# A four-layer graph network in one replayed schedule: one-hot rows partly by ScalarE, the first and last batch by halves, and a new order

## The chip, the cores and the metric

The kernel runs on one core of one Trainium2 chip. The core has five engines with queues of their own: TensorE (PE in the profile, its weight loads PEld), VectorE (DVE), ScalarE (ACT), GpSimd (POOL) and SyncE (SP). DMA transfers are issued from the queues of SP, ACT and POOL. The metric is device time in microseconds; before the change it is 2977.16 us, the median of three runs (2974.79 to 2977.79).

## The reference

There are 32 graphs (batches) of 512 nodes with 128 features, and a 0/1 adjacency of 512 x 512 per batch in which about one entry in 32 is set. Four layers follow each other, each as `x = x + layer(relu(layernorm(x)), adj)`:

```python
# layer 0: maximum over the neighbours
p = h @ (W1 - W2);  q = h @ W2
x = x + max_j( relu(p[i] + q[j] + b) * adj[i, j] )
# layer 1: four steps, each on all earlier features that it lists
src_agg = l2norm(adj, rows) @ (nodes @ ws + bs)
dst_agg = l2norm(adj, columns).T @ (nodes @ wd + bd)
nodes   = tanh(concat(src_agg, nodes @ wn + bn, dst_agg) @ wu + bu)
# layer 2
x = x + (adj / rowsum) @ (h @ weight) + bias
# layer 3: four steps of a gated unit
m = adj.T @ (h @ weight[l]);  r, z = sigmoid(...), sigmoid(...)
n = tanh(xn + r * hn);        h = (1 - z) * n + z * h
```

The output is the last x, 32 x 512 x 128 floats.

## The kernel before

**Staging.** `batch(b)` (L1222) records one batch: `load`, `prepare` (adjacency to bf16 `ab`, its transpose `at`, norms, tables), `gathers` (layer 0), `layer1` and `layer23`. Nothing is issued while it records; an object `Flow` (L279) notes each operation with its engine and what it reads and writes. Nearly every instruction of the profile is therefore issued from one line, L504, and is told apart by its tiles.

**Order.** `Flow.run` keeps up to AHEAD = 6 parts open (the three weight parts `first`, `rest`, `last`, and the batches) and issues operation by operation. Each operation has a due time: the place of its part times PACE, less the work that still depends on it, less a lead of its stage from the table LEADS (L40). Of the operations of an engine that could start first, the one with the earliest due time goes. The places of the weight parts are WEIGHTS, those of the batches their number, for the last five less LAST (L48, L1238). The result is one fixed order per engine, in which several batches lie interleaved; in the middle it repeats from batch to batch. Where the scheduler expects PE to have nothing for more than a microsecond it puts in filler matmuls (`spin`, L1232).

**Layer 0.** For each node the neighbours' rows of q are wanted. They are found in two ways: `pkey` and `top` (DVE max of eight) find up to seven of those that the second way leaves, whose rows POOL fetches from a table in HBM by indirect DMA (28 gathers a batch into `gm` and four buffers `G`), and DVE takes the maxima. The second way takes the first four neighbours in each half of a tile of 128 nodes: `ccd` holds running counts, DVE's `tensor_scalar` (L1070) makes from it a one-hot matrix `oh` of 128 x 1024 for each of four tiles (jt) and four slots (k), PE multiplies it with `qhl` into `pa` (L1073), and DVE keeps the running maximum `acc` (L1077): 16 one-hots and 32 products a batch. Then acc is transposed (`px`), joined with gm (L1080), and the layer's sum x1 is formed.

**Layer 1** (L1095): per step, `pf` transposes the features, `hi` (ACT) and `lo` (DVE) are their rounded part and the rest, `aggregate` (L910) multiplies both with at and an (the adjacency by rows), 16 matmuls of 512 columns, DVE scales the sums into `ag`, and `pu` collects the full-float products before a tanh on ACT. **Layer 2 and 3** (L1150): pg2, mT and po for layer 2; then per step of layer 3 two gates `pk` from h and from mT, the aggregate pg3 between them, phn and pxn, four operations on DVE and ACT (nn, tanh, product, sum to h), and the transposes `ph`. Every matmul, activation and vector operation here covers all 512 nodes.

**Buffers.** SBUF tiles are rings by tag: a new tile waits until the last use of the one before. PSUM's eight banks are shared by four users (`BANKS = (2, 1, 2, 1)`: layer 0's preparation, layer 1, layers 2 and 3, and the one-hot products), who keep these numbers and share the other two.

Of the kernel before, what the change touches and what calls it, by code (L numbers as in the profile page):

```python
# [32 lines left out]
CODES = ((0, 1), (P, 1), (2 * P, 2), (4 * P, 4))  # L33
NLEFT = 7
PACE = 45.28
SPACING = 1.8
AHEAD = 6
BANKS = (2, 1, 2, 1)

LEADS = {  # L40
    "prepare": -31.3, "counts": -26.1, "keys": -29.9, "rows": -0.7,
    "gather0": 21.0, "gather1": 4.8, "gather2": 6.6, "gather3": -2.7,
    "first": 14.9, "layer1": -15.8, "layer10": -31.7, "layer11": -34.7,
    "layer12": -17.6, "layer13": -49.5, "layer2": 17.3, "layer3": 7.8,
    "layer30": 58.6, "layer31": 78.0, "layer32": 36.2, "layer33": 30.6,
    "out": 18.1,
}
LAST = (0.0, 0.0, -0.31, -0.67, 0.62)  # L48
WEIGHTS = (-4.52, -3.22, -3.0)
# [548 lines left out]
class FastWeights:  # L598
# [5 lines left out]
    def __init__(self, nc, F, a, const, mid, ps):  # L604
        self.F, self.mid, self.ps = F, mid, ps
        self.NL3 = a["L3_gnn_weight"].shape[0]
        n = a["x"].shape[1]

        def fixed(shape, dtype, name):
            return const.tile(shape, dtype, name=name)  # L610

        ident = fixed([P, P], F32, "ident")
        make_identity(nc, ident)
        identb = fixed([P, P], BF16, "identb")
        nc.vector.tensor_copy(identb, ident)
        self.ident, self.identb = ident, identb
        self.mhalf = fixed([P, 8], F32, "mhalf")
        nc.gpsimd.memset(self.mhalf, -0.5)

        self.ones = fixed([P, P], F32, "ones")
        nc.gpsimd.memset(self.ones, 1.0)
        ltf = fixed([P, P], F32, "ltf")
        nc.gpsimd.affine_select(
            ltf, self.ones, pattern=[[1, P]], compare_op=ALU.is_ge, fill=0.0, base=0,
            channel_multiplier=-1,
        )
        nc.gpsimd.memset(ltf[0:HP, HP:P], 0.0)  # L630
        self.lt = fixed([P, P], F32R, "lt")
        nc.vector.scalar_tensor_tensor(self.lt, ident, NBASE, ltf, ALU.mult, ALU.add)
        self.ltk = fixed([P, P], BF16, "ltk")
        nc.vector.tensor_scalar(self.ltk, self.lt.bitcast(F32), KEY, None, ALU.mult)
        self.code = fixed([P, n // P, P], BF16, "code")
        icode, code = fixed([P, n // P], I32, "icode"), fixed([P, n // P], F32, "fcode")
        for t, (first, step) in enumerate(CODES):
            nc.gpsimd.iota(
                icode[:, t : t + 1], pattern=[[1, 1]], base=first, channel_multiplier=step
            )  # L640
        nc.vector.tensor_copy(code, icode)
        for t in range(n // P):
            nc.vector.tensor_scalar(
                self.code[:, t, :], ident, code[:, t : t + 1], None, ALU.mult
            )


        self.sign = fixed([P, 2], F32, "sign")
        nc.gpsimd.memset(self.sign[:, 0:1], -1.0)
        nc.gpsimd.memset(self.sign[:, 1:2], 1.0)  # L650
        nc.gpsimd.memset(self.sign[0:4, 0:1], 1.0)
        nc.gpsimd.memset(self.sign[0:4, 1:2], 0.0)
        self.nc, self.a, self.const, self.n = nc, a, const, n
# [32 lines left out]
    def rest(self):  # L686
# [38 lines left out]
        for i in range(NL1):  # L725
# [4 lines left out]
            for k, nm in enumerate(("ws", "wn", "wd")):  # L730
# [8 lines left out]
                F.vec.tensor_copy(wt, pt[:, 0:ch, :])  # L739
# [25 lines left out]
    def last(self):  # L765
# [14 lines left out]
        F.vec.tensor_copy(w3t, pt[:, 0:NL3, :])  # L780
        self.gh, self.gm = [], []
        for l in range(NL3):
            for nm, dst in (("hh", self.gh), ("ih", self.gm)):
# [9 lines left out]
                if nm == "hh":  # L793
                    F.vec.tensor_copy(t, pg[:, 0:3, :])
                else:
                    gt = self.temp("xn2", f"gt_{l}")[:, 0:3, :]
                    F.vec.tensor_copy(gt, pg[:, 0:3, :])
# [19 lines left out]
def fast(ctx: ExitStack, tc: tile.TileContext, a: dict, out: bass.AP, bad):  # L817
# [47 lines left out]
    def norm(s, xt, tag):  # L865
# [13 lines left out]
        xn = F.tile(mid, [P, NT, P], F32, tag=f"xn{s}", name=f"xn_{tag}")  # L879
# [14 lines left out]
    def sbuf_parts(s, src, tag):  # L894

        hi = F.tile(mid, [P, NT, P], F32R, tag=f"hi{s}", name=f"hi_{tag}")
        F.act.copy(hi, src)
        lo = F.tile(mid, [P, NT, P], F32R, tag=f"lo{s}", name=f"lo_{tag}")
# [3 lines left out]
    def parts(s, src, tag):  # L902

        hi = F.tile(mid, [P, NT, P], F32R, tag=f"hi{s}", name=f"hi_{tag}")
        F.act.copy(hi, src)
        lo = F.tile(mid, [P, NT, P], F32R, tag=f"lo{s}", name=f"lo_{tag}")
        F.vec.tensor_sub(lo, src, hi.bitcast(F32))
        return hi, lo

    def aggregate(s, two, m, name):  # L910

        pg = pst(s, name)
        hi, lo = two
        for jt in range(NT):
            F.mm(flat(pg), hi[:, jt, :], m[:, jt, :], start=(jt == 0), stop=False)
            F.mm(flat(pg), lo[:, jt, :], m[:, jt, :], start=False, stop=(jt == NT - 1))
# [3 lines left out]
    def prepare(b, xt, af):  # L920
# [16 lines left out]
        at = F.tile(big, [P, NT, N], F32R, tag="at", name=f"at_{b}", bufs=3)  # L937
# [112 lines left out]
    def gathers(b, at, ccd, qhl, pn, tab, idx, has, dinv):  # L1050
# [15 lines left out]
        for jt in range(NT):  # L1066
            F.lead = LEADS[f"gather{jt}"]
            for k in range(1, KSLOT + 1):
                oh = F.tile(big, [P, 2, N], F32R, tag="oh", name=f"oh_{b}_{jt}_{k}", bufs=3)
                F.vec.tensor_scalar(oh, ccd[jt], NBASE + k, None, ALU.is_equal)  # L1070
# [24 lines left out]
    def layer1(b, x1, an, at, dinv):  # L1095
# [14 lines left out]
        feat = {"h": hT}  # L1110
        agg = {}
        new = "h"
        for i in range(NL1):
# [3 lines left out]
            if i:  # L1117

                pt = transposed(1, feat[new], f"pf_{b}_{i}")
                two = parts(1, pt, f"{b}_1_{i}")  # L1120
            ag = F.tile(mid, [P, 2, N], F32, tag="ag" + {"f2": "f1"}.get(new, new), name=f"ag_{b}_{i}")
            for k, m in ((0, at), (1, an)):
                pg = aggregate(1, two, m, f"pg_{b}_{i}_{k}")
                F.vec.tensor_mul(ag[:, k, :], flat(pg), rbc[:, k, :])
            agg[new] = ag
            pu = pst(1, f"pu_{b}_{i}")
            F.mm(flat(pu), W.b8[:, i, :], rows, start=True, stop=False)
            late = []
            for c, nm in enumerate(names):
                F.mm(flat(pu), w[:, 1, c, :], flat(feat[nm]), start=False, stop=False)  # L1130
                for k in range(2):
                    if nm == new:
                        late.append((c, k))
                        continue
                    F.mm(flat(pu), w[:, 2 * k, c, :], agg[nm][:, k, :], start=False, stop=False)
            for c, k in late:
                F.mm(flat(pu), w[:, 2 * k, c, :], ag[:, k, :], start=False, stop=(k == 1))
# [3 lines left out]
            F.act.activation(fi, pu, AF.Tanh, bias=W.bu[:, i : i + 1])  # L1141
# [8 lines left out]
    def layer23(b, x2, an, at, dinv):  # L1150
        xn = norm(2, x2, f"{b}_2")
        two = sbuf_parts(2, xn, f"{b}_2")
        F.pool.tensor_add(x2, x2, W.b2.unsqueeze(1).to_broadcast([P, NT, P]))
        pg = aggregate(2, two, at, f"pg2_{b}")
        mT = F.tile(mid, [P, NT, P], F32, tag="mT", name=f"mT2_{b}")
        F.act.copy(mT, pg)
        po = pst(2, f"po_{b}")
# [8 lines left out]
        xn = norm(2, x3, f"{b}_3")  # L1166
        two = sbuf_parts(2, xn, f"{b}_3")
        pt = transposed(2, xn, f"pt_{b}_3")
        h = F.tile(mid, [P, NT, P], F32, tag="hg", name=f"h_{b}_3")
        F.act.copy(h, pt)  # L1170
        for l in range(W.NL3):
            F.lead = LEADS[f"layer3{l}"]
            gates = []
            for k in range(2):
                pk = pst(2, f"pk_{b}_{l}_{k}")
                F.mm(flat(pk), W.gh[l][:, k, :], flat(h), start=True, stop=False)
                gates.append(pk)
            pg = aggregate(2, two, an, f"pg3_{b}_{l}")
            mT = F.tile(mid, [P, N], F32, tag="mT", name=f"mT_{b}_{l}")
            F.act.copy(mT, flat(pg))  # L1180
            for k in range(2):
                F.mm(flat(gates[k]), W.gm[l][:, k, :], mT, start=False, stop=True)
                g = F.tile(mid, [P, N], F32, tag=f"gate{k}", name=f"gate{k}_{b}_{l}")
                c = 3 * l + k
                F.act.activation(g, flat(gates[k]), AF.Sigmoid, bias=W.bsum[:, c : c + 1])
                if k == 1:

                    zc = F.tile(mid, [P, N], F32, tag="zc", name=f"zc_{b}_{l}")
                    F.pool.tensor_scalar(zc, g, -1.0, 1.0, ALU.mult, ALU.add)
                gates[k] = g  # L1190
            r, z = gates
            c = 3 * l + 2
            phn = pst(2, f"phn_{b}_{l}")
            F.mm(flat(phn), W.gh[l][:, 2, :], flat(h), start=True, stop=True)
            nn = F.tile(mid, [P, N], F32, tag="nn", name=f"nn_{b}_{l}")
            F.vec.scalar_tensor_tensor(
                nn, flat(phn), W.bhh[:, c : c + 1], r, ALU.add, ALU.mult
            )
            pxn = pst(2, f"pxn_{b}_{l}")
            F.mm(flat(pxn), W.gm[l][:, 2, :], mT, start=True, stop=True)  # L1200
            F.vec.tensor_add(nn, flat(pxn), nn)
            F.act.activation(nn, nn, AF.Tanh, bias=W.bih[:, c : c + 1])

            F.pool.tensor_mul(z, flat(h), z)
            hn = F.tile(mid, [P, NT, P], F32, tag="hg", name=f"h_{b}_{l}")
            F.vec.tensor_mul(nn, nn, zc)
            F.vec.tensor_add(flat(hn), z, nn)
            h = hn
            pt = transposed(2, h, f"ph_{b}_{l}")
            if l + 1 < W.NL3:  # L1210
                two = parts(2, pt, f"{b}_3_{l}")
        F.lead = LEADS["out"]
        xo = F.tile(mid, [P, NT, D], F32, tag="mT", name=f"xo_{b}")
# [24 lines left out]
    places = [b - LAST[max(0, b - B + len(LAST) - 1)] for b in range(B)]  # L1238
# [474 lines left out]
```

## Time and profile before

| what | value |
|---|---|
| median of three runs | 2977.16 us |
| the profiled execution | 2976.68 us, its span 2975.0 us |
| PE busy | 2861.7 us, 96% of the span |
| DVE busy | 2393.3 us, 80% |
| ACT busy | 1216.1 us, 41% |
| POOL busy | 1819.8 us, 61% |
| filler matmuls among PE's | 257, 69.7 us |
| HBM read and written | 164.32 and 17.96 MB |

How to read it: the groups of instructions give operation, output and inputs by the names in the program, with the shapes; the timelines give start, duration, engine, operation and, in brackets, how long the engine sat idle before and what ended it. Durations of PE's matmuls overlap, so the distance of two starts says what one costs. The windows give the busy time of each engine in a stretch, in the order PE, PEld, DVE, ACT, POOL, then the granted clock of PE as a share, the DMA engines' share and GB/s.

### The profile page before, as it was taken

The numbers are of one execution on the slowest core, as the hardware profiler recorded it, in microseconds if no ns is written. First come the engines' busy times: TensorE is split into PE (matmuls) and PEld (weight loads), VectorE is DVE, ScalarE is ACT, GpSimd is POOL, SyncE is SP. The second block draws the span as 40 slices with busy tenths as digits, with TensorE's granted clock in tenths as the row PEclk, the third lists the DMA queues.
The fourth block names the chain that finished last, engine by engine and source line by source line (L and its number), as shares of the span: only waits on it lengthen the run. The fifth ranks groups of instructions, "written<-read, shape, count | busy, mean of one in ns | idle before, by whom it ended". The sixth has DMA issues, their size and how long they took to land.

```text
span 2975.0 us, 37664 instructions
## 1 busy us (share of the span) xinstructions
PE 2861.7 (96%) x11490; PEld 1752.8 (59%) x11490; DVE 2393.3 (80%) x5363; ACT 1216.1 (41%) x2528; POOL 1819.8 (61%) x2005
## 2 busy tenths in 40 slices
PE   7789999999999999999999999999999999999997
PEld 4455556666666666666666666666666666655553
DVE  6978878988888898888889888888988888887532
ACT  3333434434444443444444344444434444433322
POOL 3666766666666666666666666666666666654411
PEclk9989999999999999999999999999999999999999
DMA  7553334334334333333443333344333334321200
GB/s 171 109 94 71 63 76 86 82 74 83 62 65 85 86 78 77 75 65 69 86 86 78 78 74 65 70 85 86 77 79 74 64 72 85 67 54 43 33 4 5
DMA packets 191266, 218.43 MB, mean 73 GB/s; under 512 B 30376, under 2 KB 139600, under 8 KB 191056
## 3 DMA queue, kind: packets, MB, share of 16 engines
q0 software_dynamic: 47104, 92.34, 22.5%
q1 hardware_dynamic: 73768, 63.63, 7.3%
q10 hardware_dynamic: 70184, 59.98, 6.5%
q8 instruction: 93, 1.52, 0.2%
q14 instruction: 117, 0.96, 0.1%
HBM read 164.32 MB, written 17.96 MB: 61 GB/s over the span
## 4 chain that ended last, share of the span: by engine, by line
PE 78%; DVE 12%; issue 4%; DMA 2%; ACT 2%; POOL 2%; DVEq 0%; SPq 0%; ACTq 0%; POOLq 0%
PE pg L504 23%; PE pu L504 18%; PE pk L504 15%; PE pa L504 6%; PE pxn L504 4%; PE phn L504 4%; DVE acc L504 3%; PE pkey L504 2%; PE ph L504 2%; PE pf L504 1%; DVE nn L504 1%; DVE qhl L504 1%; PE pt L504 1%; DVE oh L504 1%; DVE x L504 1%
## 5 line engine op out<-in xcount | busy, mean ns | idle before, releaser
L504 POOL DMA_INDIRECT G<-qtab,idx x768 | 840.8, 1095 | 574.5 <-DVE gm L504 461.5
L504 DVE TENSOR_TENSOR acc<-acc,pa 128x512 f32<-128x512 f32 x992 | 673.6, 679 | 146.3 <-PE pa L504 134.2
L504 PE MATMUL pa<-oh,qhl 128*128 128x512 f32 x1024 | 472.1, 512 | 10.8 <-DVE acc L504 6.6
L504 PE MATMUL pg<-an,hi 128*128 128x512 f32 x1024 | 458.8, 448 | 2.0 <-DVE lo L504 1.6
L504 PE MATMUL pu<-ag,w 128*128 128x512 f32 x896 | 449.3, 595 | 1.5 <-DVE ag L504 1.3
L504 PE MATMUL pg<-an,lo 128*128 128x512 f32 x1024 | 432.8, 424 | 0.0
L504 DVE TENSOR_SCALAR oh<-ccd 128x1024 fp32r<-128x1024 bf16 x512 | 392.2, 783 | 13.6 <-PE pa L504 12.6
L504 PE MATMUL pg<-at,lo 128*128 128x512 f32 x640 | 296.7, 464 | 0.6 <-POOL lo L504 0.5
L504 PE MATMUL pg<-at,hi 128*128 128x512 f32 x640 | 287.7, 449 | 6.9 <-ACT hi L504 3.2
L504 PEld LDWEIGHTS pa<-oh,qhl 128*128 128x128 f32 x1024 | 194.2, 191 | 143.9 <-issue 43.6
L504 DVE TENSOR_TENSOR gm<-gm,G 128x128 f32<-128x128 f32 x768 | 258.6, 338 | 5.5 <-DMA G<-qtab,idx 4.6
L504 PE MATMUL pk<-h,g_hh 128*128 128x512 f32 x512 | 258.4, 608 | 1.8 <-ACT h L504 1.1
L504 ACT ACTIVATE xn<-x,shift,rstd 128x128 f32<-128x128 f32 x512 | 211.6, 484 | 107.5 <-POOL shift L504 107.5
L504 PEld LDWEIGHTS pg<-an,hi 128*128 128x128 f32 x1024 | 192.7, 188 | 97.0 <-issue 49.0
L504 PEld LDWEIGHTS pg<-an,lo 128*128 128x128 f32 x1024 | 193.0, 188 | 85.9 <-issue 42.0
L504 PE MATMUL pk<-mT,g_ih 128*128 128x512 f32 x512 | 241.7, 594 | 1.1 <-ACT mT L504 1.1
L504 PEld LDWEIGHTS pu<-ag,w 128*128 128x128 f32 x896 | 169.5, 190 | 118.1 <-issue 82.8
L504 ACT ACTIVATE gate<-pk,bsum 128x512 f32<-128x512 f32 x256 | 175.7, 686 | 147.8 <-PE pk L504 144.5
L504 POOL TENSOR_TENSOR rstd<-rstd,mhalf 128x4 f32<-128x4 f32 x128 | 144.1, 1126 | 138.0 <-DVE shift L504 135.9
L504 ACT COPY mT<-pg 128x512 f32<-128x512 f32 x160 | 93.7, 586 | 328.3 <-PE pg L504 324.0
L504 DVE TENSOR_TENSOR ag<-pg,rbc 128x512 f32<-128x512 f32 x256 | 174.5, 683 | 42.8 <-PE pg L504 39.7
L504 ACT CAST hi<-ph 128x512 fp32r<-128x512 f32 x96 | 56.3, 586 | 365.2 <-PE ph L504 362.2
(169 smaller groups left out, 5135.2 us busy)
## 6 DMA issues: line engine op xcount, KB each, us to landing
af<-in_adj_dram ACTq DMA_DIRECT2D x32, 1024.0 KB
ccd<-cc SPq DMA_DIRECT2D x512, 64.0 KB
an<-in_adj_dram POOLq DMA_DIRECT2D x128, 256.0 KB, 3.7
x<-in_x_dram ACTq DMA_DIRECT2D x64, 256.0 KB
rbc<-scal SPq DMA_DIRECT2D x32, 512.0 KB
G<-qtab,idx POOLq DMA_INDIRECT x768, 3.8
qtab<-qn SPq DMA_DIRECT2D x128, 64.0 KB
out_dram<-xo ACTq DMA_DIRECT2D x32, 256.0 KB
```

Source lines behind the costliest of these rows:

```text
L504: op.fn(*(real(v) for v in op.args), **{k: real(v) for k, v in op.kw.items()})
```

## The change

- **One-hots.** In batches 0, 1 and 2, the last two, two and one of the four slots of each tile are made on ACT by two activations (`far = |ccd - (64 + k)|`, then `relu(1 - far)`) instead of one DVE operation.
- **Weights.** Four kinds of copies out of PSUM in the weights' preparation go from DVE to ACT.
- **Halves.** Layer 1 of the first and the last batch, and layer 3 of the last, work in two halves of 256 nodes: the aggregates, the products, the activations and the vector operations are cut in two; the aggregate still sums over all nodes.
- **Buffers.** The last batch's tiles of layers 2 and 3 lie in tags of layer 0 (table LATE), its `at` in the tag of `af`, and its PSUM tiles count as those of user 0. BANKS becomes (1, 1, 2, 1).
- **Order.** PACE, all LEADS, LAST and WEIGHTS are new, and the first three batches are shifted by FIRST.

```diff
+ONACT = (2, 2, 1, 0)
-PACE = 45.28
+PACE = 45.33
-BANKS = (2, 1, 2, 1)
+BANKS = (1, 1, 2, 1)
 LEADS = {
-    "prepare": -31.3, "counts": -26.1, "keys": -29.9, "rows": -0.7,
-    "gather0": 21.0, "gather1": 4.8, "gather2": 6.6, "gather3": -2.7,
-    "first": 14.9, "layer1": -15.8, "layer10": -31.7, "layer11": -34.7,
-    "layer12": -17.6, "layer13": -49.5, "layer2": 17.3, "layer3": 7.8,
-    "layer30": 58.6, "layer31": 78.0, "layer32": 36.2, "layer33": 30.6,
-    "out": 18.1,
+    "prepare": -25.4, "counts": -39.2, "keys": -29.6, "rows": -14.9,
+    "gather0": 7.4, "gather1": -2.0, "gather2": -7.1, "gather3": -19.7,
+    "first": 4.7, "layer1": -35.8, "layer10": -41.4, "layer11": -66.8,
+    "layer12": -31.3, "layer13": -62.8, "layer2": 19.7, "layer3": 106.4,
+    "layer30": -29.1, "layer31": 140.3, "layer32": 106.2, "layer33": 6.1,
+    "out": -31.3,
 }
-LAST = (0.0, 0.0, -0.31, -0.67, 0.62)
-WEIGHTS = (-4.52, -3.22, -3.0)
+FIRST = (0.49, 0.03, 0.25, 0.0)
+LAST = (0.0, -0.55, 0.49, -2.35, -2.71)
+WEIGHTS = (-2.59, -2.36, -5.92)
+
+LATE = {
+    "xn2": ("xn0", 1), "hi2": ("qn", 1), "lo2": ("gm", 1), "mT": ("acc", 1), "hg": ("hT0", 1),
+    "gate0": ("pn", 2), "gate1": ("ccd", 6), "zc": ("ccd", 6), "nn": ("ccd", 6),
+}
...
-                F.vec.tensor_copy(wt, pt[:, 0:ch, :])
+                F.act.copy(wt, pt[:, 0:ch, :])
...
-        F.vec.tensor_copy(w3t, pt[:, 0:NL3, :])
+        F.act.copy(w3t, pt[:, 0:NL3, :])
...
-                    F.vec.tensor_copy(t, pg[:, 0:3, :])
+                    F.act.copy(t, pg[:, 0:3, :])
...
-                    F.vec.tensor_copy(gt, pg[:, 0:3, :])
+                    F.act.copy(gt, pg[:, 0:3, :])
...
-    def aggregate(s, two, m, name):
+    def aggregate(s, two, m, name, c=slice(0, NT)):
 
         pg = pst(s, name)
+        out = flat(pg if c.stop - c.start == NT else pg[:, 0 : c.stop - c.start, :])
         hi, lo = two
         for jt in range(NT):
-            F.mm(flat(pg), hi[:, jt, :], m[:, jt, :], start=(jt == 0), stop=False)
-            F.mm(flat(pg), lo[:, jt, :], m[:, jt, :], start=False, stop=(jt == NT - 1))
+            v = m[:, jt, c.start * P : c.stop * P]
+            F.mm(out, hi[:, jt, :], v, start=(jt == 0), stop=False)
+            F.mm(out, lo[:, jt, :], v, start=False, stop=(jt == NT - 1))
         return pg
...
-        at = F.tile(big, [P, NT, N], F32R, tag="at", name=f"at_{b}", bufs=3)
+        home = ("af", 1) if b == B - 1 else ("at", 3)
+        at = F.tile(big, [P, NT, N], F32R, tag=home[0], name=f"at_{b}", bufs=home[1])
...
-                F.vec.tensor_scalar(oh, ccd[jt], NBASE + k, None, ALU.is_equal)
+                if k > KSLOT - ONACT[min(b, len(ONACT) - 1)]:
+
+                    far = F.tile(big, [P, 2, N], BF16, tag="far", name=f"far_{b}_{jt}_{k}")
+                    F.act.activation(far, ccd[jt], AF.Abs, bias=W.slot[:, k : k + 1])
+                    F.act.activation(oh, far, AF.Relu, bias=W.ones[:, 0:1], scale=-1.0)
+                else:
+                    F.vec.tensor_scalar(oh, ccd[jt], NBASE + k, None, ALU.is_equal)
...
+        step = NT // 2 if b in (0, B - 1) else NT
+        cuts = [slice(t, t + step) for t in range(0, NT, step)]
...
+            for j, c in enumerate(cuts):
+                for k, m in ((0, at), (1, an)):
+                    pg = aggregate(1, two, m, f"pg_{b}_{i}_{k}_{j}", c)
+                    F.vec.tensor_mul(
+                        ag[:, k, cols[j]], flat(cut(pg, slice(0, step))), rbc[:, k, cols[j]]
+                    )
...
     def layer23(b, x2, an, at, dinv):
+        own = dict(LATE) if b == B - 1 else {}
+        s = 0 if own else 2
...
+        step = NT // 2 if own else NT
+        cuts = [slice(t, t + step) for t in range(0, NT, step)]
...
+                F.vec.tensor_add(cut(nn, c), vx, cut(nn, c))
+                F.act.activation(
+                    cut(nn, c), cut(nn, c), AF.Tanh, bias=W.bih[:, n : n + 1]
+                )
+
+                F.pool.tensor_mul(cut(z, c), cut(h, c), cut(z, c))
+                F.vec.tensor_mul(cut(nn, c), cut(nn, c), cut(zc, c))
+                F.vec.tensor_add(cut(hn, c), cut(z, c), cut(nn, c))
+                for t in range(c.start, c.stop):
+                    F.tr(pt[:, t, :], hn[:, t, :], W.ident)
...
-    places = [b - LAST[max(0, b - B + len(LAST) - 1)] for b in range(B)]
+    places = [
+        b - FIRST[min(b, len(FIRST) - 1)] - LAST[max(0, b - B + len(LAST) - 1)] for b in range(B)
+    ]
```

## The prediction, made blind

> **What bounds the kernel now.** I read the page's busy line first, then stretches of the span, then the timelines of the two ends.
>
> ```profile
> PE 2861.7 (96%) x11490; PEld 1752.8 (59%) x11490; DVE 2393.3 (80%) x5363; ACT 1216.1 (41%) x2528; POOL 1819.8 (61%) x2005
> L528 PE MATMUL spin<-code,identb 128*128 128x512 bf16 x257 | 69.7, 408 | 8.2 <-DVE code L643 5.4 <-DVE acc L504 2.7
> ```
>
> PE is busy 96%, but 257 of its matmuls are fillers (spin) that compute nothing. Stretches, columns: window, width, PE, PEld, DVE, ACT, POOL busy, granted clock, DMA share, GB/s:
>
> ```profile
> 0.00:45.00 45.00, 32.41 (x172) 18.24 (x173) 19.39 (x58) 17.32 (x54) 6.25 (x31) 0.92 0.59 171
> 45.00:110.00 65.00, 50.74 (x268) 30.26 (x267) 60.68 (x142) 19.83 (x51) 46.35 (x52) 0.92 0.79 148
> 110.00:175.00 65.00, 55.07 (x223) 30.89 (x222) 58.95 (x138) 19.93 (x46) 43.29 (x49) 0.92 0.50 101
> 1500.00:1600.00 100.00, 98.67 (x388) 60.51 (x386) 87.11 (x186) 43.24 (x91) 65.49 (x73) 1.00 0.41 85
> 2793.00:2894.00 101.00, 98.28 (x332) 54.83 (x332) 38.62 (x85) 33.42 (x59) 22.78 (x25) 1.00 0.04 10
> 2894.00:2966.00 72.00, 59.82 (x217) 29.12 (x215) 21.21 (x55) 18.09 (x31) 13.78 (x15) 0.98 0.02 6
> ```
>
> Three regimes. In the middle PE sets the pace: the output of one batch follows the last by 86.95 us (821.85 to 908.80 in the DVE timeline). From 45 to 175 us DVE is the full engine (93 and 91%), ACT stands at 30%. At the end only one dependent chain is left. Full-rate steps of matmuls (start to start in the timeline) are 0.23 us for 512 columns in rounded float, 0.86 for 512 in full float (two records); with them the program holds about 2,672 us of real PE work, so some 300 of the 2,975 are lost: about 128 before 400 us, 4 to 5 in each 100 us of the middle, 50 in the last 185.
>
> The start in the timelines of ACT and DVE (start, duration):
>
> ```profile
> 9.10 0.40 ACTq L504 DMA_DIRECT2D af<-in_adj_dram  x1
> 16.18 0.29 DVE L504 TENSOR_TENSOR shift<-b0r,low 128x128 f32<-128x128 f32 x1 [10.79 <-ACT low L504]
> 21.55 0.29 DVE L504 COPY wt<-pwt 128x128 f32<-128x128 f32 x1 [2.10 <-PE pwt L504]
> 21.75 2.28 DVE L504 SCALAR_TENSOR_TENSOR junk<-af 128x2048 bf16<-128x2048 f32 x1
> 44.57 0.17 DVE L504 TENSOR_SCALAR idx<-row 128x28 int32<-128x28 int32 x1
> 109.45 0.68 DVE L504 TENSOR_TENSOR gm<-gm,px 128x512 f32<-128x512 f32 x1
> 174.85 0.68 DVE L504 TENSOR_TENSOR gm<-gm,px 128x512 f32<-128x512 f32 x1
> ```
>
> The adjacency of batch 0 is asked for at 9.10, its first use on DVE stands behind weight copies; batch 0's neighbour maximum ends at 109.45, batch 1's at 174.85. The end, PE's timeline:
>
> ```profile
> 2893.19 0.66 PE L504 MATMUL px<-ident,f 128*128 128x128 f32 x4 [0.35 <-ACT f L504]
> 2894.12 4.48 PE L528 MATMUL spin<-code,identb 128*128 128x512 bf16 x20
> 2914.88 1.98 PE L504 MATMUL pk<-h,g_hh 128*128 128x512 f32 x4 [0.38 <-ACT h L504]
> 2956.42 1.98 PE L504 MATMUL pk<-mT,g_ih 128*128 128x512 f32 x4 [0.28 <-ACT mT L504]
> 2959.10 2.75 PE L528 MATMUL spin<-code,identb 128*128 128x512 bf16 x12
> 2962.68 0.63 PE L504 MATMUL ph<-ident,h 128*128 128x128 f32 x4 [0.83 <-DVE h L504]
> ```
>
> Layer 2 of batch 31 takes 21 us (2893.9 to 2914.9) with almost nothing beside it, then four steps of layer 3 take 12.0 us each.
>
> **Part 1, the start: 20 us off (8 to 30).**
> Off DVE go the copies of weights (12 wt, 1 w3t, 4 gt, 4 g_hh: 0.2 to 0.6 us a step, 8.1 us in all) and 20 one-hots (8, 8, 4 in batches 0, 1, 2; consecutive starts in this stage are 0.60 apart: 12 us). Adding up the DVE instructions in the built order with their steps from the timeline, what stands ahead of batch 0's last neighbour maximum falls from 76.7 to 53.4 us (31 instead of 40 running maxima, 8 instead of 24 one-hots); ahead of batch 1's from 134.3 to 108.0, batch 2's 183.2 to 162.1, batch 3's 240.0 to 215.4, batch 4's 299.3 to 280.6. About 20 us less DVE work stays off.
> The path: af is now the first transfer on ACT's queue, ahead of ten weight transfers; on SP four weight transfers of 64 to 192 KB move ahead of w12, which `low` needs. ACT's first operation was held to 14.58 by its own queue and I leave it there; low and shift then stay near 16, and junk follows shift at once: 16.5 instead of 21.75, 5 us. The indices came at 44.57 behind junk of batch 1 (2.28), three one-hots (1.9) and two copies (0.8), which now stand later: 34.5, 10 us earlier in all. From there to the maximum took 64.9 us around 58.7 of DVE steps; now 42.8 stand there, and the 28 gathers become the limit. They took 55 us between issues; with four buffers and 5.2 us to landing (the DMA view of 40 to 110 us) a round of four needs about 7 us: 8 issues at 1.35 and 20 at 1.7, and one landing, 50 us. So the maximum comes at 85 instead of 109, and batch 1's, some 60 us of gathers later, near 148 instead of 175.
> ACT gains 40 operations on 128x1024: no row has that shape. Below, the gate on 512 elements (0.69); above, two of them (1.37); near twice, less one overhead, 1.05: 42 us over 200, with 8 of copies on the 30% it has. The 20 pairs fit beside DVE's running maxima, which they feed; priced at 1.37 they still do. If ACT answers late, PE's pa waits and the maxima behind it.
> How much of the 24 us reaches the end: PE is not full until batch 2 is under way, so its stages move up with the maxima; but waits on PE itself and the half clock (clock 0.92 above) also lie there. I take 20; the ends are 5 to 8 (the gathers hold) and 30.
>
> **Part 2, the end: 19 us off (8 to 26).**
> In the built order the transposes that open layer 2 of batch 31 (px) now stand before the last two steps of layer 3 of batch 30, which have buffers of their own beside it. PE work behind that point: 49.2 us, it was 33.8. The 15.3 us of batch 30 now lie inside the 21 us of batch 31's layer 2, which stretches a little as PE alternates: 2 us lost, 13 won.
> Halves in layer 3: a step is 7.4 us of PE and 4.6 of waiting. The 0.72 between aggregate and pk goes (the other half's aggregate, 1.0 us, covers it); the four operations between pxn and ph (0.70, 0.73, 0.90, 0.70 and their gaps, 3.3 in the chain) run on 256 columns; the qn row, 0.42 for 256 against 0.68, makes that 1.9. That would be 2.1 a step, but the order shows 7, 13, 7, 11 fillers between pxn and ph where 11, 12, 12, 12 stood: two steps hardly improve. I take 2 us twice and 0.7 twice, 5.4.
> Check by fillers: behind batch 31's neighbour maximum 111 stood, now 49; 12 fillers went with a hole of 3.4 us, so 62 fewer are 17 us. At the low end the halves give nothing and the overlap 8.
> Cost of halves on PE: full-float ones halve exactly (pq, 256 columns, 216 ns a record against 429). Rounded ones: nearest is the 128x128 transpose, each with its own weights, 0.109 a step; I price a half at 0.123, 0.016 us more per whole: 160 of them 2.6 us, b8 and the rest to 5.9, two thirds of it in holes. I charge 2. Upper end 0.23 per half, no gain at all from halving: 37 us more PE work, of which some 15 would show.
> TensorE: Matmul & The Clock Gate, Part 3 (The mechanism), says that weight loads run beside matmuls only in other row groups. By it each half would add a load of 107 ns (same page, LDWEIGHTS), an estimate of 34 us for 320 halves, and the time would come near 2955. The trace disagrees: loads of 188 ns sit inside steps of 0.23, and transposes with new weights each follow at 0.109.
>
> **Part 3, the middle: 5 us off (25 off to 20 on).**
> The leads and PACE reorder every batch; the work is the same (DVE 66.5 us of steps per batch in both). PE has 2.5 to 4 us of holes per batch. Work between producer and consumer in the built orders, per batch: pf after pu in step 0, 0.7 to 1.3 us; pk after pt, 0.7 to 1.1 (it stalled 0.2); ph after pxn in the last step, 5.6 to 7.2 (a stall of 0.75 stood before ph); against that px after pu 1.7 to 1.3, ph after pxn in the others 0.2 to 0.4 shorter. Nothing falls below its chain (f 0.68 and a semaphore). I take 0.2 us a batch over 25; the ends are 1 us a batch gained and 0.8 lost.
>
> **Sum.** 2976.7 (the profiled execution: span 2975.0 and 1.7 around it; 0.5 under the median of the runs shown) - 20 - 19 - 5 + 2 = 2934.7. I say 2936.
>
> **Rivals.**
> A, *the gathers or the transfers hold the start.* For it: DMA stands at 0.79 from 45 to 110, and POOL waits for landings. Against: most of its waits for a gather are for DVE's gm. Start 6 instead of 20: 2949.
> B, *the middle's new order loses.* The one case that ends slower: a stall between pxn and ph (DVE and ACT answer later behind other operations) in each batch. It decides from (20 + 19 - 2) / 25 = 1.5 us a batch; at 2.5 the sum is 2976.7 - 37 + 62.5 = 3002. Against: no filler stands in the middle of the new order, as in the old, and the distances are like.
> C, *the chain of the last batch stays as long* because both halves go through DVE one by one and batch 30's work delays it. Tail 8: 2946.
> D, *everything holds and the middle gains 1 us a batch*: 2915.
>
> **How the numbers follow.** Forecast 0.50, A 0.15, B 0.11, C 0.12, D 0.09, no change by losses that cancel 0.03. The range 2910 to 2968 leaves out most of B and a little of the rest. Under 0.2% (6 us) the runs, 3 us apart, cannot tell from no change; by it faster 0.86, same 0.03, slower 0.11.
>
> **What would show it.** Right: junk of batch 0 before 18 us, its neighbour maximum near 85, batch 1's near 150, DVE under 85% in 45 to 175, about 192 fillers; px of batch 31 with xo of batch 30 20 us later; layer 3 steps of 10 to 11.3. Wrong: an unchanged 109 (gathers), batches more than 88 us apart in the middle (order), or steps of 12 at the end (halves).

## The result and the profile after

The changed kernel is slower: 3000.04 us, median of four runs (2997.48 to 3001.75), against 2977.15 (2974.79 to 2977.79) for the kernel before beside it; the ratio is 1.0078 (1.0060 to 1.0095). The forecast was 2936; a middle that loses, the outcome of its rival B, is what came. The profiled execution took 2999.38 us, its span 2997.7: 22.7 more than the span before.

Where the time lies is read from the outputs. `xo` on DVE is the last work of a batch. Its first instruction for batches 3 and 24, from DVE's timeline of the changed kernel (start, duration):

```profile
555.02 0.35 DVE L511 SCALAR_TENSOR_TENSOR xo<-ph,mcol,x 128x128 f32<-128x128 f32 x1
2424.46 0.35 DVE L511 SCALAR_TENSOR_TENSOR xo<-ph,mcol,x 128x128 f32<-128x128 f32 x1
```

The same two of the kernel before:

```profile
561.13 0.60 DVE L504 SCALAR_TENSOR_TENSOR xo<-ph,mcol,x 128x128 f32<-128x128 f32 x2
2386.02 0.60 DVE L504 SCALAR_TENSOR_TENSOR xo<-ph,mcol,x 128x128 f32<-128x128 f32 x2
```

Over the 21 batches between, that is 89.02 us a batch instead of 86.90: 2.12 us lost in each. Cut at the outputs of batches 2 and 24:

| part | before | after | difference | forecast |
|---|---|---|---|---|
| start to xo of batch 2 | 472.3 | 466.8 | -5.5 | -20 |
| from there to xo of batch 24 | 1913.7 | 1957.7 | +44.0 | -5 |
| from there to the end of the span | 589.0 | 573.2 | -15.8 | -19, and +2 for halves on PE |

The end did what was said, the start a quarter of it, and the middle has the wrong sign. The start's 5.5 is uncertain by some 3 us: in two other traces with the same starts (`tail` and `notail` below) the first row is 474.9 for the old one and 465.7 for the new. The page and the windows of the changed kernel, with the columns of the prediction's windows:

```profile
PE 2864.6 (96%) x11706; PEld 1783.8 (60%) x11725; DVE 2388.7 (80%) x5363; ACT 1272.8 (42%) x2622; POOL 1850.4 (62%) x2018
```

```profile
45.00:110.00 65.00, 49.92 (x267) 30.72 (x271) 47.05 (x116) 45.13 (x94) 42.25 (x53) 0.95 0.86 162
110.00:175.00 65.00, 54.86 (x300) 40.05 (x303) 55.22 (x134) 41.20 (x74) 43.58 (x47) 0.97 0.49 101
1500.00:1600.00 100.00, 97.25 (x383) 59.45 (x382) 85.63 (x185) 40.76 (x83) 62.78 (x69) 1.00 0.35 70
```

The page's busy shares barely move: 96% for PE in both. The loss is seen in the third window: 97.25 instead of 98.67 us of PE and 383 instead of 388 matmuls in 100 us. Which waits these are, from the waits of PE between 600 and 2340 us (engine, tile, whom it waited for: us in total, times, longest). The changed kernel:

```profile
PE pq L511 <- DVE acc L511: 11.4, 19, 0.6
PE po L511 <- DVE x L511: 10.1, 19, 0.9
PE px L511 <- DVE acc L511: 6.7, 20, 2.0
PE pk L511 <- ACT mT L511: 5.2, 20, 0.3
PE ph L511 <- DVE h L511: 4.6, 19, 0.3
PE pu L511 <- DVE acc L511: 1.8, 3, 0.6
```

The kernel before, the whole list:

```profile
PE ph L504 <- DVE h L504: 10.9, 18, 0.6
PE po L504 <- DVE x L504: 10.3, 20, 0.5
```

Before, 21.2 us in 20 batches, about 1.06 a batch; after, 40.0 in 19.5, about 2.05. New are pq, px and pu behind the running maximum `acc`, 1.0 us a batch together; px reads acc, but pq and pu don't: by the program they can wait for it only as the last reader of a PSUM bank that they are to get. pq is a tile of user 0, whose own banks BANKS cut from two to one. Waits under DVE's name rose from 1.06 to 1.77 us a batch, a third of the loss; ACT's mT has 0.27, and the rest, a little over 1 us, lies in gaps too small for the list. PE waits less at ph than before (4.6 instead of 10.9).

Why DVE is late can be seen inside one batch. The changed kernel, DVE's timeline and then POOL's in the same stretch:

```profile
1438.23 2.46 DVE L511 TENSOR_TENSOR gm<-gm,G 128x128 f32<-128x128 f32 x1
1440.61 1.46 DVE L511 TENSOR_TENSOR acc<-acc,pa 128x512 f32<-128x512 f32 x2
...
1451.25 1.36 DVE L511 TENSOR_TENSOR gm<-gm,G 128x128 f32<-128x128 f32 x1
1452.54 0.67 DVE L511 TENSOR_TENSOR acc<-acc,pa 128x512 f32<-128x512 f32 x1
```

```profile
1438.61 0.60 POOL L511 DMA_DIRECT2D an<-in_adj_dram  x1
1439.21 1.31 POOL L511 TENSOR_TENSOR gate<-h,gate 128x512 f32<-128x512 f32 x1
...
1450.52 1.95 POOL L511 TENSOR_TENSOR lo<-xn,hi 128x512 fp32r<-128x512 f32 x1 [2.41 <-ACT hi L511]
```

A maximum `gm` with a gathered row block, both operands in SBUF, takes 0.28 us as a rule (median 282 ns). Here one took 2.46 and ended at 1440.69, just behind POOL's product of gate and h (1440.52); the other took 1.36 beside POOL's `lo`, which itself took 1.95 where 1.28 is its usual (the median). The acc behind it starts at 1452.54, and PE stands idle, from its timeline:

```profile
1453.27 1.13 PE L511 MATMUL pq<-wqp,hT 128*128 128x256 f32 x4 [0.63 <-DVE acc L511]
```

I added up, from 500 to 2400 us, what `gm` and the one-hots `oh` took above their usual 0.28 and 0.68 us in all instances over 0.15 us too long: 3.4 us a batch before, 5.0 after. POOL's gate product or `lo` ran beside 95% of it before and 89% after. The longest are regular: in that stretch all 64 `gm` of over 1 us (20 before, 44 after) ended 0.15 to 0.16 us behind a gate product or a `lo`, and 40 of them had started ahead of it.

The Trainium skill, SBUF — State Buffer, section "Who interferes with whom", says that a DVE operation with two SBUF inputs and a GpSimd operation that reads SBUF exclude each other for a whole instruction; `gm`, with two inputs in SBUF, and `oh`, by the page one of the operations that can take both port pairs, are the ones that stretch here, and the acc beside them, with one input in PSUM, keeps its 0.67 to 0.69. That agrees for these operations; the operations of the POOL experiment below do not fit the "whole instruction" (last section).

### The profile page after: what moved, and what is told of

It is laid out like the page before. It is cut to its first block, busy times and chain, and to the rows that moved or that the text cites. A ratio compares the mean times of both kernels' runs of the same rounds, so it can differ in the third digit from the quotient of the medians.

```text
span 2997.7 us, 38258 instructions
## 1 busy us (share of the span) xinstructions
PE 2864.6 (96%) x11706; PEld 1783.8 (60%) x11725; DVE 2388.7 (80%) x5363; ACT 1272.8 (42%) x2622; POOL 1850.4 (62%) x2018
## 5 line engine op out<-in xcount | busy, mean ns | idle before, releaser
L511 PE MATMUL pg<-an,hi 128*128 128x512 f32 (+1 forms) x1072 | 471.2, 442 | 1.1 <-ACT hi L511 0.5
L511 PE MATMUL pu<-ag,w 128*128 128x512 f32 (+1 forms) x952 | 445.3, 568 | 0.1
L511 PE MATMUL pg<-an,lo 128*128 128x512 f32 (+1 forms) x1072 | 440.9, 414 | 0.2 <-DVE lo L511 0.2
L511 PE MATMUL pg<-at,hi 128*128 128x512 f32 (+1 forms) x672 | 293.8, 439 | 7.0 <-DVE acc L511 1.5
L511 PE MATMUL pg<-at,lo 128*128 128x512 f32 (+1 forms) x672 | 285.3, 426 | 1.9 <-DVE lo L511 1.7
L511 ACT ACTIVATE gate<-pk,bsum 128x512 f32<-128x512 f32 (+1 forms) x264 | 177.0, 674 | 189.4 <-PE pk L511 185.8
L511 PE MATMUL pk<-h,g_hh 128*128 128x512 f32 (+1 forms) x528 | 255.0, 589 | 0.5 <-ACT h L511 0.2
L511 PE MATMUL pk<-mT,g_ih 128*128 128x512 f32 (+1 forms) x528 | 244.3, 584 | 6.3 <-ACT mT L511 6.2
L511 POOL DMA_INDIRECT gm<-qtab,idx x128 | 191.0, 1492 | 73.2 <-DVE bad L511 44.6
L511 DVE SCALAR_TENSOR_TENSOR nn<-phn,bcol,gate 128x512 f32<-128x512 f32 (+1 forms) x132 | 96.6, 732 | 141.7 <-ACT gate L511 132.5
```

Of the source, the lines that this page charges most:

```text
L511: op.fn(*(real(v) for v in op.args), **{k: real(v) for k, v in op.kw.items()})
```

## The experiments

All edits of the middle hold the order of every engine: the scheduler sees the whole operation, and only what is issued is smaller (`held` and its like replace the function after it has been noted). "Distance" is the mean between the outputs of batches 3 and 24, as above; the control is the same cut in the kernel before. The kernels of the first three experiments were run once each, those with the acc cut or the POOL cut alone beside a kernel before of 2972.61 us, the others beside one of 2984.97; so times of different pairs are not to be compared to a few us. Distances repeat better: the old order gave 86.90, 86.89 and 86.85 in the kernel before and two kernels further below, the new one 89.02, 88.93 and 88.74 in the changed kernel and two others. Differences under 0.3 us a batch are not told apart here.

**DVE made lighter, in both orders.** The edit, in both kernels:

```diff
+    def held(op, n, b):
+        if b < 3:
+            return
+        at = F.part[-1]
+        at.fn = lambda out, x, y: op(*(v[..., 0:n] for v in (out, x, y)))
...
                         F.vec.tensor_max(acc, acc, flat(pa))
+                        held(nc.vector.tensor_max, 256, b)
```

> The changed kernel in its own order on every engine; from batch 3 on the running maxima acc cover 256 of the 512 columns, which leaves half of the one-hot neighbours' maxima out: 31 operations a batch of 0.42 instead of 0.68 us, 8 us of DVE less. Theory (DVE answers late in the new order, and PE waits for the PSUM banks and the h that it owes): the distance of two outputs in the middle falls from 88.8 to 87.0 or less, and the time to 2950 or less. Rival (ACT's copies, or the order on PE by itself): it stays at 88.3 to 88.8, the time within 15 us of 3000. Rival (POOL's two-operand operations stretch single DVE operations, whatever DVE's load): between, 87.8 to 88.4.

> The same cut of the running maxima in the kernel before, its own order held: the control. If DVE is late in the new order only, this gains little: the distance goes from 86.95 to 86.0 to 86.9 (PE's waits with DVE's name are 1.05 us a batch here, 1.8 in the changed kernel). If DVE's load sets the pace in both, it falls by as much as the changed kernel's, 2 us or more.

Measured: 2949.91 us with a distance of 86.95 (89.02 without the cut), and in the control 2940.34 with 85.66 (86.90). The outputs of batches 3 and 24 of the changed kernel now come here:

```profile
553.08 0.35 DVE L511 SCALAR_TENSOR_TENSOR xo<-ph,mcol,x 128x128 f32<-128x128 f32 x1
2378.95 0.35 DVE L511 SCALAR_TENSOR_TENSOR xo<-ph,mcol,x 128x128 f32<-128x128 f32 x1
```

Its list of PE's waits in the same stretch:

```profile
PE po L511 <- DVE x L511: 10.6, 20, 0.9
PE ph L511 <- DVE h L511: 5.0, 20, 0.3
PE px L511 <- DVE acc L873: 2.6, 2, 1.7
```

The waits of pq and pu behind acc are gone, and so are 2.07 us a batch: DVE was late. But the control gains 1.24, more than expected, so the old order leans on DVE too, and a gap of 1.29 between the orders is left that 8 us less of DVE do not close. The stretching of `gm` and `oh` did not shrink with it: added up as above it is 6.3 us a batch here, and 3.2 in the control. What the cut gave is room behind DVE, not fewer collisions.

**POOL's two-operand operations.**

```diff
+    def one(b):
+        if b >= 3:
+            F.part[-1].fn = lambda out, x, y: nc.gpsimd.tensor_scalar(out, x, 1.0, None, ALU.mult)
...
         F.pool.tensor_sub(lo, src, hi.bitcast(F32))
+        one(int(tag.split("_")[0]))
...
         F.pool.tensor_add(gm, gm, pn)
+        one(b)
...
         F.pool.tensor_add(x1, gm, x1)
+        one(b)
...
                 F.pool.tensor_mul(cut(z, c), cut(h, c), cut(z, c))
+                one(b)
```

> The changed kernel in its own order; from batch 3 on POOL's operations with two SBUF operands (gate times h, lo, gm plus pn, gm plus x: 9 a batch of 1.28 to 1.95 us) read one operand (0.63 us), which leaves the second terms out. If collisions of POOL and DVE on such operands make DVE late, the stretched ones go (gm with G of 1.36 and 2.46 us, lo of 1.95) and the distance falls from 88.8 to about 87.5, the time to 2965 to 2975. If DVE is late by its order alone, the distance stays above 88.4.

> The same in the kernel before, the control: if the collisions cost the new order alone, the distance stays within 0.3 us of 86.95; if they cost both alike, it falls by as much as the changed kernel's.

Measured: 2960.78 us, distance 87.27; the control 2949.55, distance 85.81. DVE issues exactly what it did, and both gain: 1.75 us a batch in the new order, 1.09 in the old. The stretching fell from 5.0 to 2.4 us a batch, and from 3.4 to 0.9. That the old order would gain nothing was wrong: both orders lose by POOL's second operands, the new one 0.66 more. The gain does not come from less work on POOL. The groups of instructions of this kernel between 600 and 2340 us (count, busy us, mean ns, idle before):

```profile
L871 POOL TENSOR_SCALAR lo<-xn 128x512 fp32r<-128x512 f32 x60 | 122.3, 2039 | 35.9 <-ACT xn L511 35.5
L871 POOL TENSOR_SCALAR gate<-h 128x512 f32<-128x512 f32 x80 | 121.5, 1519 | 4.4
```

and of the changed kernel:

```profile
L511 POOL TENSOR_TENSOR gate<-h,gate 128x512 f32<-128x512 f32 x79 | 105.3, 1333 | 3.8
L511 POOL TENSOR_TENSOR lo<-xn,hi 128x512 fp32r<-128x512 f32 x58 | 86.6, 1493 | 46.1 <-ACT hi L511 45.8
```

With one operand POOL's operations took longer (1.52 instead of 1.33 us, 2.04 instead of 1.49), not 0.63 as the expectation assumed, and the kernel was still faster. One thing more goes with the second operand: `lo` no longer waits for ACT's `hi` but for xn, as the lines show, so an earlier `lo` can have part of the gain; that is not separated.

**Both cuts, and a shorter chain in layer 3.** The third edit, in the kernels with both cuts (`short` lets a DVE operation cover the first half of the columns, `halfact` does the same for the tanh; both start at batch 3):

```diff
                 F.vec.tensor_add(cut(nn, c), vx, cut(nn, c))
+                short(nc.vector.tensor_add, P // 2, b)
                 F.act.activation(
                     cut(nn, c), cut(nn, c), AF.Tanh, bias=W.bih[:, n : n + 1]
                 )
+                halfact(b)
...
                 F.vec.tensor_mul(cut(nn, c), cut(nn, c), cut(zc, c))
+                short(nc.vector.tensor_mul, P // 2, b)
```

> The changed kernel in its own order, with both cuts from batch 3 on: the running maxima on 256 columns and POOL's two-operand operations reading one (half of the maxima and POOL's second terms are left out). Each cut alone left the new order 1.3 and 1.5 us a batch behind the old (86.95 to 85.66, 87.27 to 85.8). Theory (two causes: DVE late, and shorter distances on PE that no lighter DVE mends): the gap stays at 0.9 to 1.4 us a batch, outputs 86.2 to 86.9 apart. Rival (all of it is DVE being late, each cut mended a part): the gap falls under 0.5 us a batch, outputs 85.8 or less apart.

> The control in the order of before, both cuts: outputs 85.2 to 85.6 us apart, since little that DVE owes is left to wait for.

> As the changed kernel with both cuts, and in layer 3 from batch 3 on the sum with pxn, the tanh and the product with zc cover half of the columns, which leaves the other halves' terms out and makes the chain between pxn and ph about 0.9 us shorter in each of the four steps. Theory (what is left of the gap lies in chains that the new order gives too little work to cover, ph after h above all, 0.45 us a batch): the distance falls by 0.4 to 0.6 us more. Rival (the rest lies elsewhere, at pk behind ACT's mT and at the aggregates behind hi): it falls by less than 0.2 us.

> The control in the order of before: with both cuts its ph no longer waits, so the shorter chain brings less than 0.2 us a batch.

| cut | new order: us, distance | old order: us, distance | gap a batch |
|---|---|---|---|
| none | 2999.38, 89.02 | 2976.68, 86.90 | 2.12 |
| acc | 2949.91, 86.95 | 2940.34, 85.66 | 1.29 |
| POOL | 2960.78, 87.27 | 2949.55, 85.81 | 1.46 |
| both | 2943.17, 86.79 | 2941.97, 85.75 | 1.04 |
| both and the chain | 2924.50, 86.15 | 2935.31, 85.66 | 0.49 |

Half of the gap, 1.08, goes when DVE is light and less disturbed. Another 0.55 goes with the third edit, which gains the new order 0.64 us a batch and the old 0.09. With both cuts, PE's waits of the new order:

```profile
PE po L511 <- DVE x L511: 10.6, 20, 0.9
PE pu L511 <- DVE oh L511: 7.7, 11, 0.7
PE ph L511 <- DVE h L511: 7.0, 21, 1.1
PE pu L511 <- ACT rows L511: 2.8, 7, 1.1
```

and of the old one:

```profile
PE po L504 <- DVE x L504: 10.3, 20, 0.5
PE pu L504 <- ACT rows L504: 0.4, 1, 0.4
```

With the third edit too, the first lines of the new order's list:

```profile
PE po L511 <- DVE x L511: 10.6, 20, 0.9
PE pu L511 <- ACT rows L511: 2.1, 7, 0.9
PE ph L511 <- DVE h L511: 0.9, 1, 0.9
```

In the old order ph finds its h ready once DVE is light; in the new one it waits in every batch until the chain itself is shortened: PE's own order puts too little between pxn and ph. That is 0.3 of the 0.64 us. As much, 0.4, is pu behind DVE's oh, which is gone as well; the third edit also takes some 2.4 us of work a batch off DVE (1270 us busy between 600 and 2340, then 1231), so the 0.55 is not the chain's alone. The last 0.49 stays unassigned. Both cuts together gave no more than the acc cut alone that could be told (86.79 against 86.95); pu now waits, in the list behind oh and rows.

**The old order in the middle, and each end by itself.** The leads are chosen by batch (OLD and NEW are the two tables), PACE is that of before, and BANKS too in the middle; the rest is as in the change:

```diff
-PACE = 45.33
+PACE = 45.28
...
-BANKS = (1, 1, 2, 1)
+BANKS = (2, 1, 2, 1)
+BANKS_LATE = (1, 1, 2, 1)
...
+SWITCH = 30
+KEPT = 31
+LOW = 2
+KLOW = 6
...
+def leads(b):
+    return OLD if LOW <= b < SWITCH else NEW
...
-FIRST = (0.49, 0.03, 0.25, 0.0)
-LAST = (0.0, -0.55, 0.49, -2.35, -2.71)
-WEIGHTS = (-2.59, -2.36, -5.92)
+FIRST = (0.42, 0.39, -0.58, 0.0)
+LAST = (-0.01, -0.02, 0.33, -1.54, -4.62)
+WEIGHTS = (-2.43, -0.73, -5.57)
```

(BANKS_LATE holds up to batch KLOW and from batch KEPT.)

> The whole change, but batches 2 to 29 keep the leads of before (batches 0, 1, 30 and 31 have the new ones; BANKS is (2, 1, 2, 1) from batch 6 to 30), with which the middle comes out in the order of before; FIRST, WEIGHTS and LAST are set anew for it. Theory (the 44 us lost in the middle are the order's, the start and the end keep what they won): outputs in the middle 86.9 us apart, the neighbour maximum of batch 4 at 403 instead of 411 us, the end 10 to 16 us shorter: 2950 to 2962. Rival (something else of the change slows the middle, its buffers, the new scalar operations or the last batch's tags): outputs 88 us or more apart, 2980 or more.

Measured: 2969.69 us against 2980.96 for the kernel before beside it, ratio 0.9968 (0.9956 to 0.9980). The outputs of batches 3 and 24:

```profile
564.09 0.60 DVE L531 SCALAR_TENSOR_TENSOR xo<-ph,mcol,x 128x128 f32<-128x128 f32 x2
2388.73 0.60 DVE L531 SCALAR_TENSOR_TENSOR xo<-ph,mcol,x 128x128 f32<-128x128 f32 x2
```

The distance is 86.89: nothing of the change but its order (leads, PACE and BANKS together) slows the middle. The expected 2950 to 2962 was missed, because the start gave nothing here: batch 0's neighbour maximum came 3.6 us earlier than before (105.80), batch 3's output 3.0 us later. The end was 11.7 us shorter than before.

The second kernel, `tail`, takes the last batch's part alone, with the same LAST, the leads of before up to batch 29, PACE and BANKS of before (BANKS up to batch 30), and without one-hots on ACT, copies on ACT, FIRST or the halves of batch 0; WEIGHTS is that of before:

```diff
-ONACT = (2, 2, 1, 0)
+ONACT = (0,)
...
-        step = NT // 2 if b in (0, B - 1) else NT
+        step = NT // 2 if b == B - 1 else NT
```

> The kernel before with the last batch's part alone: halves in layers 1 and 3 of batch 31, its tiles in tags of layer 0, new LAST, the new leads for batches 30 and 31 only. Theory (this part is worth 16 us by itself and needs neither the start nor the new middle): 2977 less 10 to 16: 2961 to 2967. Rival (the end was short because the new middle left it less work over): 2973 or more.

Measured: 2969.06 us, ratio 0.9963 (0.9950 to 0.9977), 11.9 us off. It and the kernel above beat both kernels of this case; between the two there is no difference to be told, so the last batch's part is what is worth having.

The third, `notail`, is the changed kernel without that part:

```diff
-LAST = (0.0, -0.55, 0.49, -2.35, -2.71)
+LAST = (0.0, 0.0, -0.31, -0.67, 0.62)
...
-        home = ("af", 1) if b == B - 1 else ("at", 3)
+        home = ("at", 3)
...
-        step = NT // 2 if b in (0, B - 1) else NT
+        step = NT // 2 if b == 0 else NT
...
-        own = dict(LATE) if b == B - 1 else {}
+        own = {}
```

> The changed kernel with the last batch as before: no halves in it, its tiles and its at in the usual tags, LAST of before; leads, BANKS and the start are the new ones. Theory (halves, tags and LAST bring the end's 16 us): 3000 plus 12 to 18, 3012 to 3018, and the middle stays at 89.0. Rival (the new leads bring it): 3000 to 3006.

Measured: 3018.61 us, ratio 1.0131 (1.0115 to 1.0146), 18.6 more than the changed kernel, or 14.8 when each is taken from the kernel before beside it; the middle is as slow (88.93). The end's gain is that of the halves, the tags and LAST together. Where it lies, in PE's timeline of this kernel and of the changed one:

```profile
2934.49 0.66 PE L511 MATMUL px<-ident,f 128*128 128x128 f32 x4 [0.71 <-ACT f L511]
```

```profile
2915.40 0.44 PE L511 MATMUL px<-ident,f 128*128 128x128 f32 x2
...
2950.74 0.30 PE L511 MATMUL ph<-ident,h 128*128 128x128 f32 x1 [1.09 <-DVE h L511]
2962.99 0.41 PE L511 MATMUL ph<-ident,h 128*128 128x128 f32 x2 [0.44 <-DVE h L511]
2973.76 0.41 PE L511 MATMUL ph<-ident,h 128*128 128x128 f32 x2 [1.09 <-DVE h L511]
2984.96 0.41 PE L511 MATMUL ph<-ident,h 128*128 128x128 f32 x2 [0.79 <-DVE h L511]
```

From px of batch 31 to the end both need 82 us; the changed kernel gets there 19 us sooner and has the rest of batch 30 inside these 82 (its output comes at 2943.3, 28 us after px).

**The gathers of the start.**

```diff
+    def few(out, out_offset, in_, in_offset):
+        rows = bass.IndirectOffsetOnAxis(ap=in_offset.ap[0:32], axis=0)
+        nc.gpsimd.indirect_dma_start(out=out[0:32], out_offset=None, in_=in_, in_offset=rows)
...
+                if r and b < 3:
+                    at_ = F.part[-1]
+                    at_.fn = few
                 if r:
                     F.vec.tensor_max(gm[:, it, :], gm[:, it, :], G)
+                    if b < 3:
+                        F.part[-1].fn = lambda o, x, y: nc.vector.tensor_max(o[0:32], x[0:32], y[0:32])
```

> The changed kernel in its own order; in batches 0 to 2 the gathers after the first of each tile fetch 32 rows instead of 128, and the maxima with them cover those 32, which leaves the other rows' gathered neighbours out. Theory (the gathers hold the start: rival A of the prediction): batch 0's neighbour maximum falls from 99.6 to 80 to 90 us, batch 1's from 169.7 to 155 or less, the time by 5 to 15. Rival (DVE or PE hold it): batch 0's maximum at 97 or later, the time within 4 us of 2998.

Measured: 2984.24 us. Batches 0 and 1, DVE's timeline of this kernel and of the changed one:

```profile
92.81 0.69 DVE L511 TENSOR_TENSOR gm<-gm,px 128x512 f32<-128x512 f32 x1
163.06 0.67 DVE L511 TENSOR_TENSOR gm<-gm,px 128x512 f32<-128x512 f32 x1
```

```profile
99.58 0.69 DVE L511 TENSOR_TENSOR gm<-gm,px 128x512 f32<-128x512 f32 x1
169.72 0.68 DVE L511 TENSOR_TENSOR gm<-gm,px 128x512 f32<-128x512 f32 x1
```

6.8 us, between the two theories: the gathers hold a part, not the whole. 54.7 us are still needed from the indices (38.1) to the maximum. At the output of batch 3 it is 7.9 us; a further 6 us came in the middle (88.74 a batch), which I can't explain by an edit that ends with batch 2.

## Why the prediction was wrong, step by step

**Part 3, the middle: this step failed.** It took 0.2 us a batch as gained and set the worst at 0.8 lost; measured are 2.12 lost, 44.0 over the 22 batches. Three of its statements fell. "The work is the same" is true of the program and not of the engine: stretched beside POOL, DVE's `gm` and `oh` cost 5.0 instead of 3.4 us a batch above their usual. The distances counted were PE's work between producer and consumer, with each chain at its undisturbed length; acc as the last reader of a PSUM bank, on which pq and pu now wait, was not among them. And "nothing falls below its chain" holds only where DVE answers at once: in the changed kernel as it is, PE waits less at ph than before, but with a light DVE ph still waits in every batch of the new order and no longer in the old. The prediction itself had noted 0.2 to 0.4 us less in front of it.

Rival B had the outcome. Its stall between pxn and ph is not where the changed kernel waits more; it shows, with 0.3 us a batch, only when DVE is light. DVE late at the banks no case named. That its price of 3002 stands so near 3000 is luck: it took 62.5 us for the middle, where 44.0 were lost, and a start 14.5 us better than it was. Its chance of 0.11 was too low, because 25 equal stages turn a tenth of a microsecond into 2.5 us, and the harm of reordering all of them had been bounded by less (0.8 us a batch) than the waits already there came to (1.06).

**Part 1, the start: too large by 14.5 us.** (Maxima are given by their starts; so is the prediction's 109.45, which it calls the end.) Junk of batch 0 was to come at 16.5 and came at 20.8. "Low and shift then stay near 16" failed. PE's timeline of the changed kernel:

```profile
10.24 8.09 PE L535 MATMUL spin<-code,identb 128*128 128x512 bf16 x24 [10.24 <-DVE code L650]
18.17 0.38 PE L511 MATMUL plow<-wsq,ones 128*128 128x128 f32 x2
```

The prediction saw that four weight transfers move ahead of w on SP, and that low needs it, but not who stands ahead of plow: 24 fillers, which begin when DVE's `code` comes at 10.24 and take 8 us (before, 14 fillers from 5.44 on, and plow at 11.19). Then the indices came at 37.65 (34.5 said), 6.9 earlier than before, and the way to the maximum took 62 us (50 said). DVE was busy for 45 us of that stretch, near the 42.8 counted, and idle for the rest, 8.7 us of it for gathered rows; the gathers, said to be the limit, are a part of it (6.8 by the cut). So the maximum came at 99.6 instead of 85, batch 1's at 169.7 instead of 148. Of the 9.9 us won there 8.7 stood at batch 4's maximum and 5.5 at the output of batch 2. The granted clock was 0.95 and 0.97 in the two windows, where it was 0.92 before; what that gave is not separated. Rival A (6 instead of 20) had the size and part of the cause. Right were the one-hots on ACT (1.15 for each of the two activations, 1.05 said) and DVE's fall to 72 and 85% in the two windows.

**Part 2, the end: right.** 15.8 us measured against 19 less 2, with the overlap that was named in place. The gain by halves in layer 3 was less: steps of layer 3 of 12.25, 10.77 and 11.20 between the first ph of each, where 10 to 11.3 were said and 12.0 stood; two of three improve.

**Halves on PE: right.** Rounded halves of an aggregate, each with weights of its own, follow each other in PE's timeline like this:

```profile
2954.57 0.28 PE L511 MATMUL pg<-an,hi 128*128 128x256 f32 x1
2954.69 0.28 PE L511 MATMUL pg<-an,lo 128*128 128x256 f32 x1
2954.81 0.28 PE L511 MATMUL pg<-an,hi 128*128 128x256 f32 x1
```

That is 0.12 a step, where 0.123 was said. A weight load in front of each half that no matmul covers, by the rule and the 107 ns weighed in the prediction, would make it 0.23. Fillers fell from 257 to 173 in the trace (192 were said for the program).

## What to carry to other kernels

In a kernel that repeats a stage 25 times with PE at 98.67 us of 100, a new order is an edit of the stage's every wait, and what it can lose is not bounded by the idle time that PE showed before: 2.12 us a batch went where the list had shown 1.06. List who frees each PSUM bank, and which DVE and POOL operations with two SBUF operands fall beside each other. Gains at the two ends should be taken without touching the middle, which here was possible by choosing the leads by batch. Fillers are work in a queue: what is asked for behind them waits until they are through.

## What the runs showed of the hardware

A DVE maximum of 0.28 us took up to 2.46 beside POOL's work, though it started 1.0 us before POOL's gate product did by the records. That is the rule and not the exception: all 64 maxima of over 1 us between 500 and 2400 us, in both kernels, ended 0.15 to 0.16 us behind a product or a `lo` of two operands, and 40 of them had started first. By the sentence of the page told above such a pair excludes each other for an instruction; what held the maximum before the product began (in the case shown the end of a gather's issue and an issue of `an` stand there in POOL's timeline) is not separated here. The operations with one operand that took their place in the POOL experiment were longer (1.52 against 1.33 us on 128x512) and yet stretched DVE less: of 61 maxima lengthened by over 0.15 us beside them in the changed kernel, none ended just behind one; the longest five took 1.01 to 1.02 and ended 0.73 ahead of the end of `lo`. There the measurement does not bear out an exclusion for a whole instruction. The number of operands alone does not explain it, for behind `zc`, which always had one operand, 20 lengthened maxima still ended in that trace, and 19 without the cut.

Open are the last 0.49 us a batch of the gap, and whether the leads or BANKS make the new order what it is: neither was changed alone. The waits of pq, whose user lost a bank, would fit BANKS as well as a late DVE.
